# Gate projections written over their inputs' banks, and the order of small steps around the silu group, in a fused attention and state-space kernel

## Chip, cores and metric

The kernel runs on one core of one Trainium2 chip. The metric is the time of one execution on the device in microseconds (us); the time of a version is the median of its runs. An execution recorded by the hardware profiler gives the trace that the profile is made from.

## What is computed

Eight samples of 512 channels and 48x48 = 2304 positions go through two layers, each with a group norm ahead of it and a residual around it. The reference, cut to what matters:

```python
# layer 0: x = x + attention(group_norm(x)), causal linear attention, 8 heads
Q, K = elu(Wq x) + 1, elu(Wk x) + 1
den = 1 / (sum(Q * cumsum(K)) + 1e-10)
out = (Q with causal sum of K V^T) * den
# layer 1: x = x + mamba_groups(group_norm(x)); four groups of 128 channels, one after the other
xp, z = split(u @ Wi.T)                  # 256 channels each
xs = silu(conv4(xp) + bc)
dt, Bm, Cm = split(xs @ Wx.T)            # 8, 16, 16
delta = softplus(dt @ Wdt.T + bdt)
h_t = exp(delta_t * A) * h_{t-1} + delta_t * xs_t * Bm_t    # 16 states per channel
y = (sum(h_t * Cm_t) + xs * Dp) * silu(z)
x_m = y @ Wo.T                           # then mixed with x_i by sigmoid gates of channel means
```

## The kernel before

All data is fp32. Positions are cut into six chunks of 384 columns (LC). The core of the kernel is the recurrence of layer 1. A *job* is one chunk of one group of one sample: 192 jobs, each of 8 *slots*, 1536 slots in all. A slot scans four tiles of 128 partitions by 384 positions. For each of them ScalarE (ACT) computes a *decay*, exp(delta * A), into a bank of PSUM (L819); VectorE (DVE) runs the scan over it (L830) and so frees the bank. DVE also makes most of the products delta*x*B of the next slot (L809), GpSimd (POOL) the rest (L798). POOL then multiplies by C (L846), and TensorE (PE) sums the states into yp (L853). `skip` (L787) puts xs*Dp into yp first.

Six banks of PSUM (BANKS) are shared by everything else: decays, convolutions, projections, attention. `take` gives out a bank from a list, `Banks` holds them for one generator and returns them first in, first out. `ahead(n)` emits decays until n of them are waiting for their scans or no bank is spare; after each scan n is DEPTH = 3, and ahead of the silu and softplus groups n is 5. A bank returned with `late=True` is kept for decays.

Around these slots the rest is emitted by generators that yield a time and a number of banks that they need. The unit of time is a *half*, half a slot: `beside(2k)` runs after the product of slot k and before its scans, `beside(2k+1)` after its second scan. A string like "1" means that many halves after the generator's last step; a pair (t, g) means half t and at least g halves after the last step; "1w" waits for a condition. A generator whose banks are not there is asked again in the next half. The order in which all this is emitted is the order of each engine's queue; it is fixed when the program is built.

What matters around the change:

- `Job.prepare` makes a job's inputs about nine slots ahead. `conv(h)` is four matmuls (L635) of the two halves of channels, `gate(h)` one matmul for z (L646). The *silu group* on ACT is a table load and four activations, L670, L673 (both convolutions), L674 and L675 (both gates); a table load for exp follows (L819). Before the group three banks are held, and `gate(1)` takes one more after the first is freed. Then x_proj (L681) is copied by L686, dt_proj (L694) follows, and the *softplus group* (L705): a table load, two activations, a table load back to exp.
- `chunk(m)` is one chunk of attention for 128 channels. Its steps stand at `at(j)`, j halves after `times[m]`; chunks start 16 halves apart (at least 11). Projections (L288), features on ACT (L300, L301), q on DVE (L345), k (L353), v (L359), the causal sum of k (L364), pr = q times that (L374), transposes of k and v (L381) with their copies (L385, L386), denominators (L393) and the states' sums k v^T (L398) in one bank called `both`, on DVE the reciprocal rd (L401, L402) and the sums into S (L410), rd spread out by ACT (L414) and transposed by PE (L418) into another bank, q scaled by it (L423), scores (L431), mask (L436), output (L445, L449), residual and its statistics (L452, L454).
- `statistics(b)` reads sample b in 24 pieces and takes bn_stats of each (L242); `group_norm` makes a scale and a shift from statistics, by L169 to L195 with two matmuls (L171, L186). It serves both layers.
- `pass_on` brings a stream's next input: ACT scales and norms (L596, L597, L601 or L599, L607), POOL adds (L604, L609, L612). From the second chunk of a group its step stands 30 halves ahead of the job's first slot.
- SyncE (SP) issues all loads and stores in its own order.

Of the kernel before, what the change touches and what calls it, by code (L numbers as in the profile page):

```python
# [9 lines left out]
F32 = mybir.dt.float32  # L10
# [6 lines left out]
P = 128  # L17
T = 128
LC = 384
# [30 lines left out]
def attention_then_mamba_kernel(  # L50
# [17 lines left out]
    nc = tc.nc  # L68
# [92 lines left out]

    def group_norm(stats, n, name, bufs):


        bank = Banks()
        yield "1", 1
        mv = small.tile([P, n, 2], F32, tag=f"mv{n}", name=f"mv_{name}", bufs=1)
        for ct in range(n):
            nc.vector.bn_aggr(mv[:, ct, :], stats[:, ct].rearrange("p c s -> p (c s)"))  # L169
        mean_ps = bank()  # L170
        nc.tensor.matmul(mean_ps[:, 0:n], grp, mv[:, :, 0], start=True, stop=True)  # L171
        yield "1", 0
        gm = small.tile([P, 3, n], F32, tag=f"gm{n}", name=f"gm_{name}", bufs=1)
        nc.vector.tensor_copy(gm[:, 0, :], mean_ps[:, 0:n])
        nc.vector.tensor_sub(gm[:, 1, :], mv[:, :, 0], mean_ps[:, 0:n])
        bank.free()
        if n == 1:
            nc.vector.tensor_scalar(
                gm[:, 2, :], gm[:, 1, :], gm[:, 1, :], mv[:, 0, 1:2], ALU.mult, ALU.add
            )  # L180
        else:
            nc.vector.tensor_mul(gm[:, 2, :], gm[:, 1, :], gm[:, 1, :])
            nc.vector.tensor_add(gm[:, 2, :], gm[:, 2, :], mv[:, :, 1])
        yield "0", 1
        var_ps = bank()
        nc.tensor.matmul(var_ps[:, 0:n], grp, gm[:, 2, :], start=True, stop=True)  # L186
        yield "1", 0
        nc.vector.tensor_scalar_add(gm[:, 2, :], var_ps[:, 0:n], 1e-5)
        bank.free()
        norm = small.tile([P, 3, n], F32, tag=f"norm{n}", name=f"norm_{name}", bufs=bufs)  # L190
        nc.gpsimd.tensor_tensor(norm[:, 0, :], gm[:, 2, :], power[:, 0:n], ALU.pow)
        yield "1", 0
        for i, factor in ((0, -1.0), (1, float(L))):
            for ct in range(n):
                nc.vector.tensor_scalar(  # L195
                    norm[:, 1 + i, ct : ct + 1],
                    gm[:, i, ct : ct + 1],
                    norm[:, 0, ct : ct + 1],
                    factor,
                    ALU.mult,  # L200
                    ALU.mult,
                )
        return norm
# [5 lines left out]
    def statistics(b):  # L209

        xv = x[b].rearrange("(t p) l -> p t l", p=P)
        stats = small.tile([P, 4, NC, 6], F32, tag="stats_a", name=f"stats_a{b}", bufs=1)
        if b == 0:
# [19 lines left out]
        else:  # L233
            for ct in range(4):
                for c in range(NC):
                    yield "2", 0
                    if (ct, c) == (0, 0):
                        nxt = piece(b, 0)
                    xs = nxt
                    i = ct * NC + c + 1  # L240
                    nxt = piece(b, i) if i < 4 * NC else None
                    nc.vector.bn_stats(stats[:, ct, c, :], xs)  # L242
        norms[b] = yield from group_norm(stats, 4, f"a{b}", 2)

# [23 lines left out]
    def chunk(m):  # L268
# [73 lines left out]
        ex = feature(qp, qb)  # L342
        yield at(2), 0
        q = new("q", 2)
        nc.vector.scalar_tensor_tensor(q, ex, 1.0, qp, ALU.min, ALU.add)  # L345
        bank.free()
        yield at(2, 0), 1
        kp, kb = project(1)
        yield at(3), 0
        ex = feature(kp, kb)  # L350
        yield at(4), 0
        k = new("k", 2)
        nc.vector.scalar_tensor_tensor(k, ex, 1.0, kp, ALU.min, ALU.add)  # L353
# [14 lines left out]
        if ksum is not None:  # L368
            kept = new("kept")
            nc.scalar.copy(kept[64:128], kc[64:128])  # L370
            save(ksum[:, cols], kept[64:128])
# [16 lines left out]

        yield at(12), 1
        both = bank()  # L390
# [5 lines left out]
        for i in range(more):  # L396
            for h in heads_of:
                nc.tensor.matmul(ds[h, i, :], kl[:, i, h], v[:, i, h], start=True, stop=True)  # L398
        yield at(14), 0
        rd = small.tile([P, 2 * NT], F32, tag="rd", name=f"rd_{n}", bufs=1)  # L400
# [5 lines left out]
        for i in range(more):  # L406
            if c == 0 and i == 0:
                nc.vector.tensor_copy(S[:, place[1], :], ds[:, 0, :])
            else:
                nc.vector.tensor_add(S[:, place[i + 1], :], S[:, place[i], :], ds[:, i, :])  # L410
        bank.free()
        yield at(15), 0
        rdb = new("rdb", 1, (P, 2 * NT, 64))
        nc.scalar.copy(rdb, rd.unsqueeze(2).to_broadcast([P, 2 * NT, 64]))  # L414
        yield at(16), 1
        rb = bank()[:, 0:LC].rearrange("p (i t) -> p i t", i=NT)
        for i in range(NT):
            nc.tensor.transpose(  # L418
                rb[:, i, :], rdb[:, 2 * i : 2 * i + 2, :].rearrange("p e d -> p (e d)"), ident
            )  # L420
        yield at(18), 0

# [33 lines left out]
        if c + 1 == NC:  # L456
            norm = yield from group_norm(stats, 1, f"m{b}_{o}", 8)
            flush()
            done[b, o] = norm
# [156 lines left out]
    class Job:  # L616
# [6 lines left out]
        def prepare(self):  # L623
# [19 lines left out]

            def gate(h):
                zp = bank()[:, 0:LC]
                nc.tensor.matmul(  # L646
                    zp,
                    wi[:, 256 + h * P : 256 + (h + 1) * P],
                    xi[:, c0 + 3 : c0 + 3 + LC],
                    start=True,  # L650
                    stop=True,
                )
                return zp

# [3 lines left out]
            converting.append(n)  # L658
            yield "1", 1
            xc0 = conv(0)  # L660
            yield "2", 2
            xc1 = conv(1)
            zp0 = gate(0)
            yield "1", 0
            xs = self.xs = mpool.tile([P, 2, LC], F32, tag="xs", name=f"xs_{n}")
# [4 lines left out]
            nc.scalar.activation(xs[:, 0, :], xc0, AF.Silu, bias=pv[:, 0:1])  # L670
            bank.free()
            zp1 = gate(1)
            nc.scalar.activation(xs[:, 1, :], xc1, AF.Silu, bias=pv[:, 1:2])  # L673
            nc.scalar.activation(sz[0], zp0, AF.Silu)  # L674
            nc.scalar.activation(sz[1], zp1, AF.Silu)  # L675
            converting.clear()
            bank.free(3, late=True)
            yield "1", 1
# [65 lines left out]
            for h in range(2):  # L744
                yield "1", 0
                nc.gpsimd.tensor_tensor(delta[:, h, :], delta[:, h, :], xs[:, h, :], ALU.mult)  # L746
            first = 2 * self.start
            yield "2", 0
# [208 lines left out]
    def finale(job):  # L957
# [4 lines left out]
        if job.c == NC - 1:  # L962
            yield from job.stream.pass_on()

    begun, put, counted = 0, 0, list(range(1, B))

    def begin(latest):

        nonlocal begun, put
        while counted and times[parts.index((counted[0], 0, 0))] - 64 <= half_no[0]:  # L970
            tasks.append(Task(statistics(counted.pop(0))))
# [220 lines left out]
```

## Time and profile before

| | |
|---|---|
| median of 3 runs | 9329.64 us (9327.21 to 9330.81) |
| profiled execution | 9323.3 us, its span 9321.5 us |
| granted TensorE clock | 0.948 |
| mean DMA rate | 176 GB/s |
| first scan starts | 222.5 us |
| ACT table loads ahead of L670, L705, L819 | 192, 192, 382, of 1283 ns each |

A line of the costliest groups reads: line, engine, operation, what is written and read, count, then busy time and the mean of one, then the engine's idle time just before these instructions and what ended most of it. A line of waits reads: who waited, for whom, us in total, times, longest. A line of the timeline reads: start, duration, engine, line, operation, and in brackets the idle time before it and what ended it. "DVE u L830" as a cause is the end of a scan, mostly because it frees a bank. A matmul of fp32 stands as two passes in the counts.

### The profile page before, as it was taken

The numbers are of one execution on the slowest core, as the hardware profiler recorded it, in microseconds if no ns is written. First come the engines' busy times: TensorE is split into PE (matmuls) and PEld (weight loads), VectorE is DVE, ScalarE is ACT, GpSimd is POOL, SyncE is SP. The second block draws the span as 40 slices with busy tenths as digits, with TensorE's granted clock in tenths as the row PEclk, the third lists the DMA queues.
The fourth block names the chain that finished last, engine by engine and source line by source line (L and its number), as shares of the span: only waits on it lengthen the run. The fifth ranks groups of instructions, "written<-read, shape, count | busy, mean of one in ns | idle before, by whom it ended". The sixth has DMA issues, their size and how long they took to land.

```text
span 9321.5 us, 120629 instructions
## 1 busy us (share of the span) xinstructions
PE 7735.1 (83%) x35714; PEld 3673.0 (39%) x35714; DVE 8348.4 (90%) x11640; ACT 6580.2 (71%) x12656; POOL 8080.8 (87%) x5635
## 2 busy tenths in 40 slices
PE   7888888888888888888888888888888888888865
PEld 4444444433344444443343444443333434444321
DVE  3899999999999999999999999999999999999997
ACT  3677777777777777777777777776777777777775
POOL 2788888889988898889998888888998888888998
PEclk9999999999999999999999999999999999999977
DMA  6566666667666666666766666667666666666654
GB/s 189 158 169 173 175 174 168 180 189 198 188 169 176 177 179 172 176 183 189 196 182 178 174 175 173 174 170 194 192 184 182 176 176 172 173 171 175 167 153 129
DMA packets 1002899, 1642.84 MB, mean 176 GB/s; under 512 B 138592, under 2 KB 797312, under 8 KB 1002240
## 3 DMA queue, kind: packets, MB, share of 16 engines
q1 hardware_dynamic: 1002240, 1635.13, 64.1%
q8 instruction: 283, 4.64, 0.2%
q14 instruction: 376, 3.08, 0.1%
HBM read 1309.06 MB, written 325.58 MB: 175 GB/s over the span
## 4 chain that ended last, share of the span: by engine, by line
DVE 39%; ACT 20%; PE 18%; issue 7%; DMA 7%; POOL 6%; SPq 2%; DVEq 0%; POOLq 0%; ACTq 0%
DVE u L830 23%; DVE u L809 8%; PE bank L288 7%; ACT bank L819 6%; PE bank L635 4%; POOL u L846 4%; ACT L819 3%; PE yp L853 3%; PE bank L646 2%; ACT L705 2%; DMA B<-scr 2%; DMA C<-scr 1%; ACT bank L301 1%; ACT delta L705 1%; DVE sm L436 1%
## 5 line engine op out<-in xcount | busy, mean ns | idle before, releaser
L830 DVE TENSOR_TENSOR_SCAN u<-bank,u 128x385 f32<-128x385 f32 (+1 forms) x6144 | 5475.1, 938 | 530.5 <-ACT bank L819 503.2
L846 POOL TENSOR_TENSOR u<-u,C 128x1536 f32<-128x1536 f32 x1536 | 4885.1, 3180 | 219.5 <-DVE u L830 112.6
L819 ACT ACTIVATE bank<-dr,av 128x385 f32<-128x385 f32 (+1 forms) x6144 | 3431.3, 579 | 1556.9 <-DVE u L830 1113.3
L853 PE MATMUL yp<-u,cst 128*64 128x384 f32 x12288 | 2429.9, 514 | 282.7 <-ACT yp L787 146.3
L798 POOL TENSOR_TENSOR u<-B,dxr 128x512 f32<-128x512 f32 x1536 | 1959.9, 1276 | 22.4 <-DMA dxr<-xscr 19.0
L288 PE MATMUL bank<-xn,wq_sb 128*128 128x384 f32 x4608 | 1855.1, 552 | 48.8 <-DVE u L830 31.7
L809 DVE TENSOR_TENSOR u<-B,dxp 128x1024 f32<-128x1024 f32 x1536 | 1834.7, 1195 | 10.7 <-ACT dxp L782 10.7
L853 PEld LDWEIGHTS yp<-u,cst 128*64 128x64 f32 x12288 | 788.3, 139 | 1476.6 <-issue 903.5
L635 PE MATMUL bank<-xi,wk 128*128 128x384 f32 x3072 | 1118.2, 507 | 280.1 <-ACT kl L385 172.7
L288 PEld LDWEIGHTS bank<-xn,wq_sb 128*128 128x128 f32 x4608 | 929.1, 212 | 862.9 <-issue 215.1
L635 PEld LDWEIGHTS bank<-xi,wk 128*128 128x128 f32 x3072 | 563.7, 193 | 862.2 <-ACT kl L385 254.1
L844 POOL COPY state<-u 128x4 f32<-128x4 f32 x1280 | 243.8, 190 | 740.6 <-DVE u L830 738.0
L300 ACT ACTIVATE ex<-bank,bqkv_sb 128x384 f32<-128x384 f32 x384 | 221.3, 576 | 561.6 <-PE bank L288 539.2
L787 ACT ACTIVATE yp<-xs,pv 128x384 f32<-128x384 f32 x384 | 223.4, 582 | 405.7 <-DVE yz L865 405.7
L819 ACT ACT_TABLE_LOAD x382 | 490.1, 1283 | 6.7
L746 POOL TENSOR_TENSOR delta<-delta,xs 128x384 f32<-128x384 f32 x384 | 385.8, 1005 | 95.5 <-DMA dscr<-delta 84.3
L418 PE MATMUL bank<-cst,rdb 128*128 128x128 f32 x576 | 112.7, 310 | 426.1 <-DVE u L830 334.7
L694 PE MATMUL bank<-dbc,wd 9*128 9x384 f32 x768 | 316.3, 524 | 65.1 <-ACT dbc L686 29.0
L646 PE MATMUL bank<-xi,wi 128*128 128x384 f32 x768 | 297.8, 500 | 59.8 <-ACT xs L670 59.8
L871 PE MATMUL bank<-yz,wo 128*128 128x384 f32 x768 | 297.6, 509 | 34.1 <-DVE yz L865 19.4
L449 PE MATMUL bank<-sm,v 128*64 128x128 f32 x2304 | 257.2, 301 | 42.4 <-DVE u L830 40.6
L418 PEld LDWEIGHTS bank<-cst,rdb 128*128 128x128 f32 x576 | 66.8, 153 | 558.9 <-ACT xb L601 272.5
(109 smaller groups left out, 7860.3 us busy)
## 6 DMA issues: line engine op xcount, KB each, us to landing
B<-scr SPq DMA_DIRECT2D x1536, 192.0 KB
C<-scr SPq DMA_DIRECT2D x1536, 192.0 KB
xn<-xn SPq DMA_DIRECT2D x192, 768.0 KB
dr<-dscr SPq DMA_DIRECT2D x768, 192.0 KB
dxr<-xscr SPq DMA_DIRECT2D x768, 192.0 KB
dscr<-delta SPq DMA_DIRECT2D x192, 384.0 KB
xscr<-delta SPq DMA_DIRECT2D x192, 384.0 KB
xn<-in_x SPq DMA_DIRECT2D x48, 768.0 KB
```

Source lines behind the costliest of these rows:

```text
L288: nc.tensor.matmul(ps, wq_sb[:, kt, j * 512 + o * P : j * 512 + (o + 1) * P], xn[:, kt, :], start=(kt == 0), stop=(kt == 3),)
L635: nc.tensor.matmul(xc, wk[:, k, h * P : (h + 1) * P], xi[:, c0 + k : c0 + k + LC], start=(k == 0), stop=(k == 3),)
L646: nc.tensor.matmul(zp, wi[:, 256 + h * P : 256 + (h + 1) * P], xi[:, c0 + 3 : c0 + 3 + LC], start=True, stop=True,)
L694: nc.tensor.matmul(vp, wd[32:41, h * P : (h + 1) * P], dbc[32:41, :], start=True, stop=True)
L746: nc.gpsimd.tensor_tensor(delta[:, h, :], delta[:, h, :], xs[:, h, :], ALU.mult)
L798: nc.gpsimd.tensor_tensor(u[:, :, :, 1 + LC - TAIL :], self.B[s % 4][:, :, cols].unsqueeze(2).to_broadcast(shape), self.dxr[s // 4][:, :, ...
L809: nc.vector.tensor_mul(u[:, :, :, 1 : 1 + LC - TAIL], self.B[s % 4][:, :, cols].unsqueeze(2).to_broadcast(shape), self.dxp.unsqueeze(1).to ...
L819: nc.scalar.activation(dA[:, cols], self.dr[h][:, g, cols], AF.Exp, scale=self.w[6][:, 2 * h + g, q + j : q + j + 1],)
L830: nc.vector.tensor_tensor_scan(u[:, j, g, cols], dA[:, cols], u[:, j, g, cols], 0.0, ALU.mult, ALU.add,)
L846: nc.gpsimd.tensor_tensor(h, h, self.C[s % 4].unsqueeze(2).to_broadcast([P, NG, 2, LC]), ALU.mult)
L853: nc.tensor.matmul(self.yp[g * 64 : g * 64 + 64, 0:LC], pair_sum, u[:, j, g, 1:], start=False, stop=(s % 4 == 3 and j == NG - 1), skip_gro ...
L871: nc.tensor.matmul(self.xm[:, 0:LC], self.w[2][:, h, :], self.yz[:, h, :], start=(h == 0), stop=(h == 1),)
```

## The change

The number of instructions of every engine stays as it is, and so does what they compute.

- In `prepare` the gates take no banks of their own. Gate h writes the bank of convolution h, after the silu that reads it. Both gates now stand behind the second convolution and behind their silus; two banks are held and freed in place of four. The steps of the convolutions and of the silu group stand at fixed halves (21, 19 and 18 ahead of the job's first half).
- In `chunk` the second projection is emitted ahead of the q product, which moves from half 2 to half 3; two projections then hold banks at once. The denominators and sums move from half 12 to half 10, with no gap asked, and rd and the sums into S from 14 to 12. The bank `both` isn't freed after them: the transposed rd is written over it, and it is freed after q is scaled, at half 16 in place of 18.
- Statistics of a sample (from the third on) take one piece per 16 halves, at fixed halves, over a longer time, with the load two halves ahead; for the second sample a piece per half. The statistics' tile has two buffers. The group norm of layer 1 has its steps at halves 28 to 31 of its chunk.
- `kept` shares a buffer with `before` of the attention.

```diff
-    def group_norm(stats, n, name, bufs):
+    def group_norm(stats, n, name, bufs, places=("1", "1", "0", "1", "1")):
...
-        yield "1", 1
+        yield places[0], 1
...
         else:
-            for ct in range(4):
-                for c in range(NC):
-                    yield "2", 0
-                    if (ct, c) == (0, 0):
-                        nxt = piece(b, 0)
-                    xs = nxt
-                    i = ct * NC + c + 1
-                    nxt = piece(b, i) if i < 4 * NC else None
-                    nc.vector.bn_stats(stats[:, ct, c, :], xs)
+            when = begins[b] + b % 2
+            for i in range(4 * NC):
+                yield (when - 2, 1) if b > 1 else "1", 0
+                xs = piece(b, i)
+                yield (when, 1) if b > 1 else "1", 0
+                nc.vector.bn_stats(stats[:, i // NC, i % NC, :], xs)
+                when += PERIOD
...
         ex = feature(qp, qb)
-        yield at(2), 0
-        q = new("q", 2)
+        yield at(2), 1
+        kp, kb = project(1)
+        yield at(3), 0
+        q, k = new("q", 2), new("k", 2)
         nc.vector.scalar_tensor_tensor(q, ex, 1.0, qp, ALU.min, ALU.add)
         bank.free()
-        yield at(2, 0), 1
-        kp, kb = project(1)
-        yield at(3), 0
         ex = feature(kp, kb)
...
-            kept = new("kept")
+            kept = new("before")
...
-        yield at(12), 1
+        yield at(10, 0), 1
         both = bank()
...
-        yield at(14), 0
+        yield at(12), 0
         rd = small.tile([P, 2 * NT], F32, tag="rd", name=f"rd_{n}", bufs=1)
...
-        bank.free()
-        yield at(15), 0
+        yield at(13), 0
         rdb = new("rdb", 1, (P, 2 * NT, 64))
...
-        yield at(16), 1
-        rb = bank()[:, 0:LC].rearrange("p (i t) -> p i t", i=NT)
+        yield at(14), 0
+
+        rb = both[:, 0:LC].rearrange("p (i t) -> p i t", i=NT)
...
-        yield at(18), 0
+        yield at(16), 0
...
-            norm = yield from group_norm(stats, 1, f"m{b}_{o}", 8)
+            norm = yield from group_norm(
+                stats, 1, f"m{b}_{o}", 8, [(times[m] + j, 1) for j in (28, 29, 29, 30, 31)]
+            )
...
-            def gate(h):
-                zp = bank()[:, 0:LC]
+            def gate(h, zp):
...
-            yield "1", 1
+            first = 2 * self.start
+            yield (first - 21, 0), 1
             xc0 = conv(0)
-            yield "2", 2
+            yield (first - 19, 2), 1
             xc1 = conv(1)
-            zp0 = gate(0)
-            yield "1", 0
+            yield (first - 18, 1), 0
...
             nc.scalar.activation(xs[:, 0, :], xc0, AF.Silu, bias=pv[:, 0:1])
-            bank.free()
-            zp1 = gate(1)
+
+            gate(0, xc0)
             nc.scalar.activation(xs[:, 1, :], xc1, AF.Silu, bias=pv[:, 1:2])
-            nc.scalar.activation(sz[0], zp0, AF.Silu)
-            nc.scalar.activation(sz[1], zp1, AF.Silu)
+            gate(1, xc1)
+            nc.scalar.activation(sz[0], xc0, AF.Silu)
+            nc.scalar.activation(sz[1], xc1, AF.Silu)
             converting.clear()
-            bank.free(3, late=True)
+            bank.free(2, late=True)
...
+    begins = {}
+    for b in counted:
+        first = times[parts.index((b, 0, 0))]
+        begins[b] = (first - 20) // PERIOD * PERIOD - 4 * NC * PERIOD - 2 if b > 1 else first - 64
...
-        while counted and times[parts.index((counted[0], 0, 0))] - 64 <= half_no[0]:
+        while counted and begins[counted[0]] - 4 <= half_no[0]:
```

More of the change, by code (lines that the diff above doesn't have):

```diff
@@ L171, in group_norm @@
         nc.tensor.matmul(mean_ps[:, 0:n], grp, mv[:, :, 0], start=True, stop=True)
-        yield "1", 0
+        yield places[1], 0
         gm = small.tile([P, 3, n], F32, tag=f"gm{n}", name=f"gm_{name}", bufs=1)
@@ L183, in group_norm @@
             nc.vector.tensor_add(gm[:, 2, :], gm[:, 2, :], mv[:, :, 1])
-        yield "0", 1
+        yield places[2], 1
         var_ps = bank()
         nc.tensor.matmul(var_ps[:, 0:n], grp, gm[:, 2, :], start=True, stop=True)
-        yield "1", 0
+        yield places[3], 0
         nc.vector.tensor_scalar_add(gm[:, 2, :], var_ps[:, 0:n], 1e-5)
@@ L191, in group_norm @@
         nc.gpsimd.tensor_tensor(norm[:, 0, :], gm[:, 2, :], power[:, 0:n], ALU.pow)
-        yield "1", 0
+        yield places[4], 0
         for i, factor in ((0, -1.0), (1, float(L))):
@@ L211, in statistics @@
         xv = x[b].rearrange("(t p) l -> p t l", p=P)
-        stats = small.tile([P, 4, NC, 6], F32, tag="stats_a", name=f"stats_a{b}", bufs=1)
+        stats = small.tile([P, 4, NC, 6], F32, tag="stats_a", name=f"stats_a{b}", bufs=2)
         if b == 0:
@@ L342, in chunk @@
         ex = feature(qp, qb)
-        yield at(2), 0
-        q = new("q", 2)
+        yield at(2), 1
+        kp, kb = project(1)
+        yield at(3), 0
+        q, k = new("q", 2), new("k", 2)
         nc.vector.scalar_tensor_tensor(q, ex, 1.0, qp, ALU.min, ALU.add)
         bank.free()
-        yield at(2, 0), 1
-        kp, kb = project(1)
-        yield at(3), 0
         ex = feature(kp, kb)
         yield at(4), 0
-        k = new("k", 2)
         nc.vector.scalar_tensor_tensor(k, ex, 1.0, kp, ALU.min, ALU.add)
@@ L652, in gate @@
                 )
-                return zp
             while converting or not st.scaled:
@@ L658, in prepare @@
             converting.append(n)
-            yield "1", 1
+            first = 2 * self.start
+            yield (first - 21, 0), 1
             xc0 = conv(0)
-            yield "2", 2
+            yield (first - 19, 2), 1
             xc1 = conv(1)
-            zp0 = gate(0)
-            yield "1", 0
+            yield (first - 18, 1), 0
             xs = self.xs = mpool.tile([P, 2, LC], F32, tag="xs", name=f"xs_{n}")
@@ L746, in prepare @@
                 nc.gpsimd.tensor_tensor(delta[:, h, :], delta[:, h, :], xs[:, h, :], ALU.mult)
-            first = 2 * self.start
             yield "2", 0
```

## Prediction

> **What bounds the kernel now.** I read the busy shares first, then what VectorE (DVE) waited for in the steady part, then the timeline around one such wait. Of the page, the shares and the costliest group:
>
> ```profile
> PE 7735.1 (83%) x35714; PEld 3673.0 (39%) x35714; DVE 8348.4 (90%) x11640; ACT 6580.2 (71%) x12656; POOL 8080.8 (87%) x5635
> L830 DVE TENSOR_TENSOR_SCAN u<-bank,u 128x385 f32<-128x385 f32 (+1 forms) x6144 | 5475.1, 938 | 530.5 <-ACT bank L819 503.2
> ```
>
> DVE is the bound: 8348 of 9321.5 us. The change moves DVE work but adds and removes none (the built order of both kernels has 11,450 DVE instructions), so the time can only move through the 973 us in which DVE idles. The waits of DVE between 230 and 9300 us name the idle time (total us, times, longest):
>
> ```profile
> DVE u L830 <- ACT bank L819: 503.2, 194, 4.7
> DVE q L345 <- ACT bank L301: 108.1, 54, 4.2
> DVE k L353 <- ACT bank L301: 56.0, 135, 1.0
> DVE gm_m L188 <- PE bank L186: 29.4, 31, 1.1
> ```
>
> There are 192 jobs and 194 waits of a scan for its decay: one per job, 2.6 us each. One of them, on ScalarE (ACT), then DVE, then TensorE (PE):
>
> ```profile
> 4054.83 0.58 ACT L819 ACTIVATE bank<-dr,av 128x385 f32<-128x385 f32 x1 [0.26 <-DVE u L830]
> ...
> 4055.54 1.28 ACT L670 ACT_TABLE_LOAD   x1
> 4056.84 0.58 ACT L670 ACTIVATE xs<-bank,pv 128x384 f32<-128x384 f32 x1
> ...
> 4058.42 0.49 ACT L675 ACTIVATE sz<-bank 128x384 f32<-128x384 f32 x1
> ...
> 4060.23 2.10 ACT L819 ACTIVATE bank<-dr,av 128x385 f32<-128x385 f32 x4
> ...
> 4067.87 1.28 ACT L705 ACT_TABLE_LOAD   x1
> ...
> 4071.35 0.59 ACT L819 ACTIVATE bank<-dr,av 128x385 f32<-128x385 f32 x1
> 4074.67 0.58 ACT L300 ACTIVATE ex<-bank,bqkv_sb 128x384 f32<-128x384 f32 x1 [2.73 <-PE bank L288]
> ```
> ```profile
> 4057.53 0.95 DVE L830 TENSOR_TENSOR_SCAN u<-bank,u 128x385 f32<-128x385 f32 x1
> 4060.85 0.96 DVE L830 TENSOR_TENSOR_SCAN u<-bank,u 128x385 f32<-128x385 f32 x1 [2.36 <-ACT bank L819]
> ...
> 4075.73 0.56 DVE L345 SCALAR_TENSOR_TENSOR q<-ex,bank 128x384 f32<-128x384 f32 x1 [3.05 <-ACT bank L301]
> ```
> ```profile
> 4057.47 0.91 PE L646 MATMUL bank<-xi,wi 128*128 128x384 f32 x2 [0.19 <-ACT xs L670]
> 4058.22 0.72 PE L393 MATMUL bank<-cst,pr 128*128 128x2 f32 x6
> ...
> 4069.71 0.55 PE L418 MATMUL bank<-cst,rdb 128*128 128x128 f32 x3 [3.75 <-ACT delta L705]
> ```
>
> The reader is to see two chains. In the first, ACT makes no decay for 4.69 us (4055.54 to 4060.23), while DVE has only the decays made before. In the second, PE stands 3.75 us at the transposes of L418, for want of a bank; the projection queued behind them comes late, ACT waits at L300, and DVE waits at L345. The second group of this kind on ACT (softplus, 4067.87 to 4071.35, 3.48 us in every job) costs DVE nearly nothing: 0.14 us on average before its scan.
>
> **What the Trainium skill says.** "ScalarE: Activation LUTs", What ACT_TABLE_LOAD costs, gives 1283 ns for a load and about 1380 ns of drain beside it. The trace agrees on the load and shows no drain: the next activation starts 0.01 us after it, so I price a switch at 1.28 us. "PSUM — Partial Sum Buffer", Specifications, gives 8 banks and PSUM as all that TensorE writes; with dxp and yp in two, six are left, as in the code. "Perfetto Trace Analysis", Optimization Strategy, says that consistent bubbles can mean that there isn't enough PSUM. The trace agrees: the bubble is there once a job, and behind L418 stands a bank.
>
> **The rule for a group.** The last decay ahead of a group waits for the bank that an earlier scan frees. Call that scan's end R. Need is the time from R until the first decay behind the group is done; cover is the DVE work from R to the scan that takes it. DVE waits need less cover. In the built order of before, R lies four scans ahead of that scan at the silu group, in all 190 groups in the steady part. Measured over them: 6.55 us from R to the scan, 2.61 idle, so cover 3.94 (three scans of 0.86, a product of 1.12 and small ones). In its commonest form (L385 and L386 queued ahead) the need is 6.59.
>
> **Part 1, the silu group.** (a) Need. Today ACT waits for one gate only; L675 starts 1.00 us after the first silu ends in nearly all groups. In the change both gates write banks that the silus have just read. Gate 0 can't begin before the first silu ends, and gate 1 follows. A matmul of 128x384 is two passes of 0.322 us start to start (L288 and L635 back to back), so the fourth activation starts 0.64 us later. Moreover the order puts the denominators and sums (L393, L398) between the second convolution and gate 0, where today gate 0 stands. They take 1.06 us (4058.22 until L681 starts at 4059.28). The convolution starts when L385 has freed its bank, and its last pass has been issued 2.67 us later; with 1.06 gate 0 starts at 3.73. The first silu ends at 3.20, and would let it start at 3.31. That is 0.43 more. Need: 6.59 + 0.64 + 0.43 = 7.66. Bounds: 0.64 alone if PE has the sums done early, 1.5 if the gates meet a late convolution; I take 1.07. (b) Cover. R stays four scans ahead in 176 of 190. The order now has L401, L402 and the L410s in this stretch in 182 groups (0.85 us: 4061.72 to 4062.61 less gaps) and 144 pieces of bn_stats instead of 19 (0.5 each): 0.81 + 0.33 = 1.14 per group, so 5.1. (c) Wait: 7.69 (with 0.03 to the scan's start) - 5.1 = 2.6, as today. 190 x 2.6 = 492 against 495: the cover that is gained is spent on the longer group. Effect about -3 us.
>
> **Part 2, the softplus group.** Nothing in its lines changes, but its banks do. Today one bank is spare there: the sums' bank is back, and that of L418 isn't taken yet. A fourth decay lies ahead of the group, and R to the scan is five scans and two products. In the change the sums' bank is held from phase 10 until L423. With two for softplus, three decays are all that six banks hold, and the order shows R only four scans ahead in 177 of 190. Cover is a product, three scans and L423: 1.12 + 3 x 0.86 + 0.45 = 4.15. Need: the decay 0.52, then what the order queues behind it (L596, L597, L601: 0.51 + 0.51 + 0.69, all three in 110 groups, two in 30, one in 7), the group 3.48, the next decay 0.58, two handovers 0.06: 6.35, 5.66, about 5.3, or 4.64 with none (35). Waits: 110 x 2.2 + 30 x 1.5 + 7 x 1.2 + 35 x 0.5 = 312 us, less the 26 of today: +286. Bounds: the group alone, with nothing queued ahead of it, is 190 x 0.5 - 26 = +70; ACT coming 0.5 us late to that decay adds 95 to the 286, so +380.
>
> **Part 3, the second chain.** L418 writes the bank it already holds, so PE no longer stands there (L418 waited 335 us for scans, 86 for L705). The first projection's bank comes from the scan after R, two us behind R; the projection (eight passes, 2.7 us) is done near R + 4.8, and ACT comes to L300 after R + 6.4. The q product (L345) moves a slot part later too. So 108 + 56 go, and I leave 10: -154 us. Next late is ACT at the decay that stands behind L300 and L787; it is done 3.7 us after the softplus scan, and needed at 5.5. Bounds -100 and -164.
>
> **Part 4, the statistics.** The norm's L188 (29 us) moves to where DVE waits in any case: -29, or 0. The pieces' loads on SP are issued two half-slots ahead as before, among the B and C loads; today bn_stats waits 0.3 us in all after the start, in every phase. Priced at 0. If SP is blocked, up to 2 us of it falls into the silu wait. The 140 us of idle before the first scan are PE's and DMA's; +-10.
>
> **Sum.** -3 + 286 - 154 - 29 = +100 us against the profiled execution (9323.3 us, span 9321.5): 9423. The median of the runs is 6.3 higher, so 9430.
>
> **Rivals.** *Faster.* Were the softplus stretch hidden, what is left is -186: 9144. One mechanism: the decay ahead of L596 must be made from a bank free before R. It turns the sign where the new wait falls under 1.0 us a group (186 / 190) instead of 1.6. For it: today's group of the same length is hidden. Against it: the banks in the order. *About even.* The silu group takes the 0.64 alone (wait 2.16, -82 us) and some softplus waits shrink: 9335. For it: PE waits 0.8 us on average ahead of L646 today. Against: conv and silu start from the same L385, so the sums can't be done early. *Slower still.* The gates hold PE's queue, the gathers of L853 stand behind them, yp and L787 come late and hold ACT: 0.5 us more per job, 9525. Against: ACT idles 406 us at L787 today and DVE doesn't feel it.
>
> **Chances.** Forecast 0.60 (9370 to 9490 by itself), even 0.17, faster 0.13, slower still 0.10. A change of about 0.2% (19 us) is what a measurement here can tell. Slower by more: 0.60 + 0.10 + 0.02 of the even case; within: 0.11; faster: 0.13 + 0.04. The range 9320 to 9520 leaves out the faster rival and half of the slowest.
>
> **What would show it.** Right: DVE waits for L819's successor about 380 times, half of them behind a softplus group at 1.6 us; the silu waits still near 2.5 us; gate 0 late behind the sums; no wait at the q product; no PE wait at the rb transposes. Wrong: fewer than 250 such waits, or silu waits under 2 us.

## The result and the profile after

| | before | after |
|---|---|---|
| median | 9328.49 us (4 runs) | 9653.74 us (4 runs, 9645.74 to 9666.77) |
| ratio | | 1.035, 95% interval 1.0332 to 1.0368 |
| profiled execution, its span | 9323.3, 9321.5 us | 9666.8, 9665.0 us |
| DVE busy, idle | 8348, 933 us | 8388, 1237 us |
| granted TensorE clock | 0.948 | 0.926 |

The change makes the kernel 325 us slower. The forecast had the direction, and 100 us. (The idle time is the sum of the gaps ahead of DVE's instructions, the 17 us ahead of its first among them.)

The page of the changed kernel, the lines that answer to those of before (scan and decay are now L826 and L815):

```profile
PE 7992.1 (83%) x35714; PEld 3742.1 (39%) x35714; DVE 8388.3 (87%) x11640; ACT 6628.2 (69%) x12656; POOL 8074.7 (84%) x5635
L826 DVE TENSOR_TENSOR_SCAN u<-bank,u 128x385 f32<-128x385 f32 (+1 forms) x6144 | 5497.5, 939 | 668.7 <-ACT bank L815 638.2
```

What DVE waited for over the whole run:

```profile
DVE u L826 <- ACT bank L815: 638.2, 340, 2.3
DVE rd L397 <- PE bank L394: 223.3, 190, 10.4
DVE k L349 <- ACT bank L299: 117.4, 91, 3.3
DVE fg L878 <- PE bank L867: 51.2, 30, 2.3
...
DVE gm_m L188 <- PE bank L186: 13.5, 31, 3.7
...
DVE q L345 <- ACT bank L299: 7.8, 7, 3.6
```

The scans wait 340 times and not 194, at most 2.3 us at a time. Two waits are new, at the reciprocal rd (for the sums) and at fg (for the output projection), and the q waits are gone.

One job shows every term. First ACT, from the silu group (4021.73) over the softplus group (4034.72) to the k features (4049.57):

```profile
4021.73 0.58 ACT L666 ACTIVATE xs<-bank,pv 128x384 f32<-128x384 f32 x1
...
4023.89 0.49 ACT L671 ACTIVATE sz<-bank 128x384 f32<-128x384 f32 x1 [1.11 <-PE bank L643]
...
4032.48 0.58 ACT L815 ACTIVATE bank<-dr,av 128x385 f32<-128x385 f32 x1 [0.27 <-DVE u L826]
4033.00 0.60 ACT L594 ACTIVATE fu<-fu,wt 128x384 f32<-128x384 f32 x1
...
4034.72 1.28 ACT L702 ACT_TABLE_LOAD   x1
...
4038.20 1.09 ACT L815 ACTIVATE bank<-dr,av 128x385 f32<-128x385 f32 x2
...
4049.57 0.58 ACT L298 ACTIVATE ex<-bank,bqkv_sb 128x384 f32<-128x384 f32 x1 [4.42 <-PE bank L286]
```

Then DVE in the same job:

```profile
4023.06 0.17 DVE L397 TENSOR_SCALAR rd<-bank 128x6 f32<-128x6 f32 x1 [0.66 <-PE bank L394]
...
4026.95 0.96 DVE L826 TENSOR_TENSOR_SCAN u<-bank,u 128x384 f32<-128x384 f32 x1 [1.57 <-ACT bank L815]
...
4038.82 0.96 DVE L826 TENSOR_TENSOR_SCAN u<-bank,u 128x385 f32<-128x385 f32 x1 [2.23 <-ACT bank L815]
...
4050.63 0.56 DVE L349 SCALAR_TENSOR_TENSOR k<-ex,bank 128x384 f32<-128x384 f32 x1 [1.95 <-ACT bank L299]
```

And PE:

```profile
4022.94 1.56 PE L643 MATMUL bank<-xi,wi 128*128 128x384 f32 x4
...
4034.48 2.85 PE L286 MATMUL bank<-xn,wq_sb 128*128 128x384 f32 x8 [1.33 <-DVE u L826]
...
4041.41 1.65 PE L867 MATMUL bank<-yz,wo 128*128 128x384 f32 x2 [3.44 <-DVE yz L861]
4042.99 2.83 PE L849 MATMUL yp<-u,cst 128*64 128x384 f32 x8
4045.75 3.79 PE L286 MATMUL bank<-xn,wq_sb 128*128 128x384 f32 x8
```

The reader is to see a chain that the prediction didn't have. DVE waits 2.23 us behind the softplus group, so the gated y (yz) is late; PE, which reached the output projection L867 early, stands 3.44 us for it. What PE does next runs slowly: the eight matmuls of L849, which sum the states into yp, take 2.83 us, where others of them take 1.51, and the k projection takes 3.79, where the q projection of the same size took 2.85. Over the whole run PE is busy 7992 us with the same 35,714 passes that took 7735 before. So ACT gets the k projection late (4.42 us of wait) and DVE waits once more, at k.

Where DVE's idle time went, by place, summed over the profiled executions (us). A group's place reaches from the end of the scan R, as the prediction defines it (four scans ahead), to the scan that takes the first decay behind the group; waits at q, k and fg stand in a row of their own:

| place | before | after | difference | forecast |
|---|---|---|---|---|
| silu groups, with rd and the norm steps in them | 531 | 563 | +32 | -32 |
| softplus groups | 26 | 323 | +297 | +286 |
| products q, k, fg | 214 | 176 | -38 | -154 |
| all else, the start among it | 162 | 175 | +13 | 0 |
| DVE busy | 8348 | 8388 | +40 | 0 |

Idle and busy together give 344 us, the difference of the spans. The busy 40 are 18 us of longer durations and 22 us of lost overlap: two DVE instructions in a row overlap by some 0.08 us in the records, and where there is a gap between them they don't. There are some 250 gaps more, 200 of them over 0.15 us.

### The profile page after: what moved, and what is told of

It is laid out like the page before. It is cut to its first block, busy times and chain, and to the rows that moved or that the text cites. A ratio compares the mean times of both kernels' runs of the same rounds, so it can differ in the third digit from the quotient of the medians.

```text
span 9665.0 us, 120018 instructions
## 1 busy us (share of the span) xinstructions
PE 7992.1 (83%) x35714; PEld 3742.1 (39%) x35714; DVE 8388.3 (87%) x11640; ACT 6628.2 (69%) x12656; POOL 8074.7 (84%) x5635
## 4 chain that ended last, share of the span: by engine, by line
DVE 32%; ACT 22%; PE 20%; POOL 9%; issue 8%; DMA 6%; SPq 2%; DVEq 0%; POOLq 0%; ACTq 0%
DVE u L826 19%; DVE u L805 7%; ACT bank L815 7%; PE bank L633 6%; POOL u L842 5%; ACT L815 4%; PE bank L286 4%; PE yp L849 3%; PE bank L643 3%; DMA C<-scr 3%; ACT L702 2%; POOL u L794 2%; ACT delta L702 1%; DVE yz L861 1%; PE bank L867 1%
## 5 line engine op out<-in xcount | busy, mean ns | idle before, releaser
L826 DVE TENSOR_TENSOR_SCAN u<-bank,u 128x385 f32<-128x385 f32 (+1 forms) x6144 | 5497.5, 939 | 668.7 <-ACT bank L815 638.2
L815 ACT ACTIVATE bank<-dr,av 128x385 f32<-128x385 f32 (+1 forms) x6144 | 3433.3, 579 | 1561.9 <-DVE u L826 1338.2
L849 PE MATMUL yp<-u,cst 128*64 128x384 f32 x12288 | 2697.8, 549 | 157.3 <-POOL u L842 124.1
L286 PE MATMUL bank<-xn,wq_sb 128*128 128x384 f32 x4608 | 1784.9, 533 | 129.5 <-DVE u L826 100.8
L849 PEld LDWEIGHTS yp<-u,cst 128*64 128x64 f32 x12288 | 860.0, 147 | 1504.5 <-issue 979.8
L286 PEld LDWEIGHTS bank<-xn,wq_sb 128*128 128x128 f32 x4608 | 902.3, 207 | 1092.5 <-DVE u L826 376.5
L867 PE MATMUL bank<-yz,wo 128*128 128x384 f32 x768 | 376.6, 583 | 399.2 <-DVE yz L861 387.6
L815 ACT ACT_TABLE_LOAD x381 | 488.8, 1283 | 6.7
L691 PE MATMUL bank<-dbc,wd 9*128 9x384 f32 x768 | 340.4, 554 | 104.3 <-DVE u L826 70.4
L867 PEld LDWEIGHTS bank<-yz,wo 128*128 128x128 f32 x768 | 145.1, 210 | 565.0 <-DVE yz L861 486.6
L377 PE MATMUL bank<-cst,vT 128*128 128x128 f32 x576 | 102.6, 287 | 223.8 <-DVE pr L370 200.3
```

The costliest lines, as they stand in the source:

```text
L286: nc.tensor.matmul(ps, wq_sb[:, kt, j * 512 + o * P : j * 512 + (o + 1) * P], xn[:, kt, :], start=(kt == 0), stop=(kt == 3),)
L691: nc.tensor.matmul(vp, wd[32:41, h * P : (h + 1) * P], dbc[32:41, :], start=True, stop=True)
L815: nc.scalar.activation(dA[:, cols], self.dr[h][:, g, cols], AF.Exp, scale=self.w[6][:, 2 * h + g, q + j : q + j + 1],)
L826: nc.vector.tensor_tensor_scan(u[:, j, g, cols], dA[:, cols], u[:, j, g, cols], 0.0, ALU.mult, ALU.add,)
L849: nc.tensor.matmul(self.yp[g * 64 : g * 64 + 64, 0:LC], pair_sum, u[:, j, g, 1:], start=False, stop=(s % 4 == 3 and j == NG - 1), skip_gro ...
L867: nc.tensor.matmul(self.xm[:, 0:LC], self.w[2][:, h, :], self.yz[:, h, :], start=(h == 0), stop=(h == 1),)
```

## The experiments

Theory A is that the loss comes from the decay that no longer lies ahead of the softplus group. Its rivals: B, the gates hold TensorE's queue; C, the order of work in TensorE's queue makes VectorE wait; D, TensorE has no time left, whatever its order; E, TensorE runs slower after it has stood still. Ratios are to the kernel before on the same chip. Differences in us from the changed kernel are differences of medians; the kernel before measured 9325 to 9332 us beside the different runs, so some 10 us of such a difference mean nothing.

**pass_on later** (the changed kernel, with)

```diff
-                    yield (first - 30, 1), 0
+                    yield (first - 28, 1), 0
```

> The changed kernel with one edit: the ACT steps of pass_on stand 28 halves ahead of the job in place of 30, so that they are queued behind the softplus group and not ahead of it. Theory A (decays: the loss is VectorE waiting behind the softplus group, because only three decays lie ahead of it and pass_on's three activations are queued between the last of them and the group): the wait per group falls from 2.2 us (with three activations) to 0.5, 226 us in all, and about 40 us of waits that follow from it; 60 us may come back because the activations now stand ahead of another decay: 9390 to 9480 us. Theory B (TensorE: the gates hold its queue and it runs at a lower clock, and VectorE waits for what comes late from it): the order of these ACT steps matters little, 9600 to 9660 us.

Measured: 9582.77 us, ratio 1.0267 (1.0252 to 1.0283), 71 us under the changed kernel. Idle time at the softplus groups fell from 323 to 110 us, 213 of the 226 expected. But DVE waited at k more than before the edit:

```profile
DVE u L826 <- ACT bank L815: 439.3, 370, 2.3
DVE rd L397 <- PE bank L394: 223.4, 190, 10.2
DVE k L349 <- ACT bank L299: 211.1, 139, 3.4
```

So A has the wait right to 0.1 us a group, but only a third of it comes through, and the time misses A's range: behind it stands another chain.

**q scaled before the softplus group** (the changed kernel, with)

```diff
-        yield at(16), 0
+        yield at(15), 0
         nc.vector.tensor_mul(q, q, rb.rearrange("p i t -> p (i t)"))
```

> The changed kernel with one edit: q is scaled by the transposed reciprocal one half earlier, so that the bank of denominators and reciprocal is free when the softplus group is emitted, and the order has a fourth decay ahead of the group (waiting for the scaling of q). Theory A: need 6.9 us from the scan, cover about 6.6, so the softplus wait nearly goes: 270 of 308 us, 9350 to 9400 us with the waits that follow. Theory B: the granted clock and the gates are as before, 9600 to 9660 us.

Measured: 9505.65 us, 1.0183 (1.0166 to 1.02), 148 us under the changed kernel. At the softplus groups 78 us of idle time are left, 245 less. Other waits of DVE grew: at k to 140 us, at fg to 81, at L188 to 43. One bank freed some 2.2 us sooner, seen from the start of the group, is worth 1.5% here, and again not all of it arrives; A had forecast 9350 to 9400 us.

**Gates alone** (the kernel before, with)

```diff
-            def gate(h):
-                zp = bank()[:, 0:LC]
+            def gate(h, zp):
...
-            yield "2", 2
+            yield "2", 1
             xc1 = conv(1)
-            zp0 = gate(0)
...
-            bank.free()
-            zp1 = gate(1)
+            gate(0, xc0)
...
+            gate(1, xc1)
-            nc.scalar.activation(sz[0], zp0, AF.Silu)
-            nc.scalar.activation(sz[1], zp1, AF.Silu)
+            nc.scalar.activation(sz[0], xc0, AF.Silu)
+            nc.scalar.activation(sz[1], xc1, AF.Silu)
...
-            bank.free(3, late=True)
+            bank.free(2, late=True)
```

> The kernel before with one part of the change alone: the gates write the banks of the convolutions, two banks in place of four. The order now has four decays ahead of the silu group in 159 of 190 groups. Theory A: the group is 0.64 us longer (the second gate follows the first on TensorE) but the cover grows from 3.9 to 5.8 us, so the silu wait falls from 2.7 to about 1.4 us: 9329 - 250 = 9080 to 9130 us. Theory B (gates behind the silus hold TensorE's queue, and that is what costs): slower than before, 9400 us or more.

Measured: 9340.75 us, 1.0008 (0.9999 to 1.0016): no difference. B is out: the gates by themselves don't make the kernel slow. A's forecast of 9080 to 9130 us fails too. The group is 0.69 us longer on average (4.76 to 5.45), about as said. The fourth decay ahead is there, but the last of them begins only 1.2 us earlier: ACT itself is busy, copying k and v (L385, L386) right ahead of the last two decays in 121 of 190 groups. With the longer group, and 0.14 us more of cover, that leaves 0.63 us a group: 531 us of idle time became 412. Waits elsewhere took this back, mostly those at k (156 us for 71) and at rd (69, of which 41 lie within the 412).

**The sums' bank alone** (the kernel before, with)

```diff
-        bank.free()
         yield at(15), 0
...
-        yield at(16), 1
-        rb = bank()[:, 0:LC].rearrange("p (i t) -> p i t", i=NT)
+        yield at(16), 0
+        rb = both[:, 0:LC].rearrange("p (i t) -> p i t", i=NT)
```

> The kernel before with another part alone: the transposed reciprocal is written over the bank of denominators and sums, which is held until q is scaled; times as before. The order has three decays ahead of the softplus group in 180 groups in place of four. Theory A: softplus waits of about 2.7 us in 91 groups, 2.0 in 24, 1 or less in the rest, 340 us in all, less up to 160 us of waits at the q and k products, since TensorE no longer stands for a bank: 9480 to 9540 us. Theory B: the part only frees TensorE, so it gains: 9180 to 9250 us.

Measured: 9645.90 us, 1.0333 (1.0317 to 1.0348). That is nearly the whole loss, with this part alone, and 106 us more than A's range. Its waits (scan, k and q):

```profile
DVE u L829 <- ACT bank L818: 913.7, 374, 4.7
DVE k L353 <- ACT bank L301: 90.5, 99, 5.7
DVE q L345 <- ACT bank L301: 72.9, 40, 6.0
```

Idle time at the softplus groups is 412 us; in 91 of them it is 3.0 us each. PE no longer stands for a bank at the transposes, and the q waits fall by 69 us; the k waits rise by 20. The freed PE gains 50 us, not 160: it now stands at the output projection, further on in its own queue.

```profile
PE bank L870 <- DVE u L829: 310.6, 159, 2.9
...
PE bank L870 <- DVE yz L864: 102.9, 138, 4.0
```

**k projection ahead of the output projection** (the changed kernel, with)

```diff
         qp, qb = project(0)
+        yield at(0, 0), 1
+        kp, kb = project(1)
         yield at(1), 0
         ex = feature(qp, qb)
-        yield at(2), 1
-        kp, kb = project(1)
         yield at(3), 0
```

> The changed kernel with one edit: the second projection is emitted right behind the first, one and a half slots earlier, so that on TensorE it stands ahead of the output projection, which waits for the gated y. Theory C (order on TensorE: freed from its wait at the transposes, TensorE now stands 2.4 us per job at the output projection, with the k projection queued behind it, and VectorE pays at the k product): the k waits fall from 117 us to under 30 and the wait of the output projection from 388 us to under 200: 9530 to 9580 us. Theory D (TensorE has no time left, whatever its order): k waits go down but waits at other products come in their place, 9630 to 9670 us.

Measured: 9641.19 us, 1.0335 (1.0318 to 1.0353), 13 us under the changed kernel. The k waits are gone, and fg waits 154 us for 51. TensorE stands 67 us for yz at the output projection and not 388; it stands at the scores (L427, 413 us). C is right about who waits behind whom, and wrong about what it is worth: the wait got another name, and the time lies in D's range.

**Sums behind the gates** (the changed kernel, with)

```diff
-        yield at(10, 0), 1
+        yield at(11, 0), 1
         both = bank()
...
-        yield at(12), 0
+        yield at(13), 0
         rd = small.tile([P, 2 * NT], F32, tag="rd", name=f"rd_{n}", bufs=1)
...
-        yield at(13), 0
+        yield at(14), 0
         rdb = new("rdb", 1, (P, 2 * NT, 64))
...
-        yield at(14), 0
+        yield at(14, 0), 0
         rb = both[:, 0:LC].rearrange("p (i t) -> p i t", i=NT)
```

> The changed kernel with the denominators and sums emitted one half later, behind the gates, and the reciprocal and sums on VectorE one half later too. Theory A: the silu group on ScalarE is 0.45 us shorter (5.89 to 5.44), since gate 0 no longer waits for the sums; and as the sums' bank is taken later, the order has a fourth decay ahead of the group, cover 7.2 us against a need of about 8.0: the idle time of VectorE per silu group falls from 3.0 to about 1.1 us. 350 us less, of which up to 100 may come back at the k product: 9300 to 9400 us. Rival (as in the gates-only run, ScalarE is late itself, and the waits are only renamed): the group is shorter, but the time falls by less than 120 us.

Measured: 9394.49 us, 1.0069 (1.0053 to 1.0084), 259 us under the changed kernel. The time lies in A's range, and its rival is out. The silu group takes 5.40 us for 5.89; its idle time falls from 563 to 320 us, and the softplus groups keep theirs (some 350 us). What is left at the silu groups over the forecast of 1.1 us each is in two waits for TensorE in this stretch, rd and the norm's mean:

```profile
DVE u L826 <- ACT bank L815: 350.7, 202, 3.4
DVE rd L397 <- PE bank L394: 144.2, 150, 4.2
DVE gm_m L174 <- PE bank L171: 103.1, 30, 4.0
```

**Norm steps as before** (the changed kernel, with)

```diff
-            norm = yield from group_norm(
-                stats, 1, f"m{b}_{o}", 8, [(times[m] + j, 1) for j in (28, 29, 29, 30, 31)]
-            )
+            norm = yield from group_norm(stats, 1, f"m{b}_{o}", 8)
```

> The changed kernel with the steps of the layer 1 group norm as before. Theory C: the variance matmul (L186) no longer takes a bank that the softplus group holds, so TensorE doesn't stand 200 us there, and the 52 us in which VectorE waits at the fg product (30 times about 1.7) go; up to 29 us may come back at L188: 9590 to 9640 us. Rival: the fg waits come from the output projection's wait in every job, and stay; within 20 us of the changed kernel.

Measured: 9676.63 us, 1.0371 (1.0356 to 1.0387), 23 us over the changed kernel. The fg waits are gone (1 us), as C said, but the rd waits grew from 223 to 319 us, and the time misses C's range. Taking the later norm steps away gains nothing here.

**TensorE kept busy** (the changed kernel, with three matmuls ahead of each output projection whose results nobody reads)

```diff
             self.xm = self.bank()
+            for _ in range(3):
+                nc.tensor.matmul(self.xm[:, 0:LC], ident, cst[:, 0:LC], start=True, stop=True)
```

> The changed kernel with three matmuls more ahead of every output projection, into the bank that the projection then overwrites: 576 matmuls of 128x384 that compute nothing needed, about 1.9 us of TensorE per job, placed where it stands waiting. Theory E (the clock: standing for two to three us lowers TensorE's rate for what follows, and that is what makes the k projection late): the k waits fall from 117 to about 60 us, the k projection takes 2.9 us and not 3.8, and the time falls by 30 to 80 us: 9570 to 9620 us. Theory D (TensorE has no time left): the added work comes through as later projections, k and fg waits grow, 9700 us or more.

Measured: 9628.54 us, 1.0320 (1.0305 to 1.0335): 25 us faster than the changed kernel with 576 matmuls more, 9 us outside E's range. The granted clock went from 0.926 to 0.948, and TensorE's stands for yz at the output projection from 388 us to 107. DVE at fg and k, in that kernel:

```profile
DVE fg L880 <- PE bank L869: 121.2, 43, 4.1
...
DVE k L349 <- ACT bank L299: 17.3, 10, 3.3
```

The k waits went from 117 to 17 us, further than E had it, and 70 us came back at fg. By D, which has no time left on TensorE, the kernel would have been slower: D is out. The rate can be read in the traces. Taking two successive passes of 384 columns of one line, the time between their starts, by the length of TensorE's last stand and the time since it ended:

```
kernel           stands of 2.5 to 4 us    passes 0-3 us after    passes 8 us and more after
before                     73                 0.63 to 0.64              0.322
changed                   136                 0.63 to 0.69              0.322
kept busy                  52                 0.63 to 0.69              0.322
(medians in us; after stands of 1 to 1.5 us, 0.32 throughout, in all three)
```

The border isn't sharp. Of the passes within 3 us after stands of 2 to 2.5 us, 32% were over 0.5 us apart before, 58% in the changed kernel and 7% in the one kept busy.

**The rest alone** (the kernel before, with the order of the q product, the spread statistics, the later norm steps and the shared buffer of the change; the steps of the convolutions as before)

> The kernel before with what is left of the change when the gates and the sums' bank stay as before: the second projection ahead of the q product, the pieces of statistics spread out, the group norm's later steps, the shared buffer. Theory A+C: bn_stats gives the silu group 0.33 us more cover (60 us), L188 no longer waits (25 us), and the q waits (142 us) turn partly into k and fg waits; no decay is lost: 9180 to 9290 us. Rival (the loss is spread over all parts): slower than before, 9350 us or more.

Measured: 9356.01 us, 1.0030 (1.0019 to 1.0042), 31 us slower, where a gain of 40 us and more was forecast. The q waits went from 142 to 20 us, fg rose from 1 to 103, and a wait of the norm for POOL (L195) from 1 to 38. The idle time at the silu groups fell by 22 us, but only because L188 (29 us) no longer waits there. The scan's own wait rose from 496 to 505 us, though 132 pieces of bn_stats stand in that stretch and not 18.

**All but the sums' bank** (the changed kernel, with)

```diff
-        yield at(10, 0), 1
+        yield at(12), 1
         both = bank()
...
-        yield at(12), 0
+        yield at(14), 0
...
+        bank.free()
-        yield at(13), 0
+        yield at(15), 0
...
-        yield at(14), 0
-        rb = both[:, 0:LC].rearrange("p (i t) -> p i t", i=NT)
+        yield at(16), 1
+        rb = bank()[:, 0:LC].rearrange("p (i t) -> p i t", i=NT)
...
-        yield at(16), 0
+        yield at(18), 0
```

(with the convolutions' steps relative to each other, as before)

> The changed kernel without its part on the sums' bank: gates, projections, statistics and norm steps as in the change; denominators, sums, reciprocal and its transposes at the times and in the banks of before. Theory A: the loss of the change lies in this one part; gates alone were +8 us, the rest alone as in the run beside it, and the two add up: within 40 us of that run, 9170 to 9300 us. Rival (the parts hurt each other): 9400 us or more.

Measured: 9319.34 us, 0.9994 (0.9988 to 1.0001). Without this part the change costs nothing: taking it away gains 334 us, more than the whole loss of 325. (The time is over A's range of 9170 to 9300, but within 40 us of the run beside it, as A said.) Gates (+8), sums' bank (+313) and the rest (+31), each alone, add to 352; the parts nearly add up. What was taken away here is two things, the bank held until q is scaled and the sums a half or more earlier, ahead of the gates, and these two don't add: the bank alone costs 313 us in the kernel before, sums behind the gates give 259 in the changed one, and both together give 334.

**Three mends together** (the changed kernel with the sums behind the gates, q scaled at half 15, norm steps as before: the diffs above)

> The changed kernel with three edits together: sums behind the gates and the reciprocal one half later (9394 us alone), q scaled one half earlier so that a fourth decay lies ahead of the softplus group (148 us alone), group norm steps as before. Theory A: the first two add up, less what returns at the k and fg products: idle time at the softplus groups under 100 us, 9230 to 9300 us. Theory D (TensorE is what limits there): the waits are renamed once more, 9380 us or more.

Measured: 9310.07 us, 0.9985 (0.9978 to 0.9992), 344 us under the changed kernel, and 0.15% under the kernel before. Idle time at the softplus groups is 54 us, at the silu groups 346. A had forecast 9230 to 9300 us and D 9380 or more; the time lies just over A's range. DVE now waits most at

```profile
DVE k L349 <- ACT bank L299: 265.7, 173, 3.6
DVE rd L397 <- PE bank L394: 251.2, 176, 6.2
```

**Three mends, TensorE kept busy** (the same, with the three matmuls)

> The kernel of the run beside it with three matmuls more ahead of every output projection, which compute nothing needed. Theory E (clock): where TensorE stands less before the k projection, VectorE waits less at the k product, as in the changed kernel, where it gave 26 us: 20 to 80 us faster than the run beside it. Theory D: 20 us or more slower.

Measured: 9237.82 us, 0.9901 (0.9887 to 0.9916), 72 us faster than the run beside it. Its k waits are a third of that one's:

```profile
DVE rd L397 <- PE bank L394: 261.9, 177, 6.7
DVE k L349 <- ACT bank L299: 90.0, 141, 3.6
DVE fg L878 <- PE bank L867: 84.2, 84, 5.5
```

The granted clock is 0.970. It is the fastest version, 1% under the kernel before, and 72 of these 87 us come from work that computes nothing. E forecast 20 to 80 us.

## Why the prediction was right or wrong

**Where the forecast missed.** It had +100 us for the spans, which differ by 344. Of the 244 between them 116 lie in part 3, 64 in part 1 with the norm's credit, 40 in DVE's busy time, which had no term, 13 in all else and 11 in part 2.

**Part 2, softplus: right.** By what is queued between the last decay and the group, the forecast had waits of 2.2, 1.5, 1.2 and 0.5 us; the trace has 2.21 (110 groups), 1.63 (30), 1.22 (7) and 0.49 (30). The part forecast +286 and measured +297. The run of the sums' bank alone and the run without it show that this edit carries the loss.

**Part 3, the second chain: failed.** The step was "Next late is ACT at the decay that stands behind L300 and L787", with the q and k waits gone. Next late was TensorE itself. Its waits, before and then in the changed kernel:

```profile
PE bank L418 <- DVE u L830: 334.7, 149, 2.8
...
PE bank L418 <- ACT delta L705: 86.2, 28, 3.8
...
PE bank L871 <- DVE yz L865: 19.4, 10, 2.4
```
```profile
PE bank L867 <- DVE yz L861: 387.6, 159, 4.7
PE bank L633 <- ACT kl L381: 240.0, 164, 1.6
```

Where it had stood 421 us at the transposes for scans and L705, it now stands 388 us for the gated y, in front of the k projection; that wait was 19 us. In the run of the sums' bank alone 414 us stand at the same place. The prediction followed the q projection as far as ACT and never asked what lies behind it in TensorE's own queue. Then the rate: behind a stand of more than 2.5 us most passes of the next 3 us come at half rate, and there were some 150 such stands for some 85. The Trainium skill has a halving of this kind ("TensorE: Matmul & The Clock Gate", What's actually happening: the clock is halved after an idle window of about 3.4 us and needs as long a busy one to come back). The passes at 0.634 us for 0.322 agree; here they came already after stands of 2.5 to 4 us, and in part after 2 to 2.5. The prediction used 0.322 everywhere. Together: q -134, k +46, fg +50, in all -38 for -154.

**Part 1, silu: the mechanism right, the sizes short.** The wait "as today" was 2.6 us; DVE is idle 3.0. Over the 176 groups in which R lies four scans ahead, the need, forecast at 7.69 us from the end of scan R to the scan behind the group, measured 7.95. The group is 5.89 where 5.75 was forecast, and the last decay ahead of it starts 0.85 after R, not 0.72. The cover is 4.96, not 5.1. Of the 527 us of idle time of these groups 183 stand at rd, where DVE waits for the sums, which the forecast counted as work. The decay comes later still, so these waits should cost nothing by themselves; no run tests that. It does split the wait: the scan itself waits 1.84 us on average, which by the words of the prediction ("silu waits under 2 us") was a sign of being wrong. The credit of 29 us at L188 came in only in part: L188 still waits 13.5 us, and the norm's mean (L174) went from 2.4 to 8.8. Together this makes +32 for -32.

**Part 4 and the sum.** Statistics cost nothing that the runs show, as priced; in the run of the rest alone they gained nothing either, where 60 us were expected of them. Not in the sum at all were the 40 us of DVE busy time, more than half of them overlap lost, and the start (rd waits 32 us there).

**Rivals.** "Slower still" looked at the right place, TensorE's own queue, with the wrong carrier: it had the gates hold the queue, and the gates alone cost nothing. The "even" and "faster" cases fell with the fourth decay, as the order had said.

What stays open: how much of the k and fg waits is the rate and how much the order. The two runs with added matmuls show that the rate matters (25 and 72 us). How far a version without stands would go was not tried, and neither were the added matmuls in the kernel before. The fixed places of the convolutions' steps were never run by themselves: the runs of the gates, the sums' bank and the rest alone, and the run without the sums' bank, all have them as before.

## What to carry to other kernels

Count banks by how long they are held, not by how many a step takes: a bank kept across a table switch takes a buffer away from the engine that must be ahead there, and the built order shows it before any run. When a wait of an engine goes, read on in that engine's own queue to the next thing that waits, and ask what it holds up; here the two edits that took the softplus wait away gave a third and three fifths of it (71 of 213 us, 148 of 245), since DVE's next waits grew. Time a stage by its stretch of need against cover: that gave the softplus waits to 0.13 us or better.

## What the runs showed of the hardware that had not been expected

- TensorE ran at half rate after standing: fp32 passes of 384 columns came 0.634 us apart for 0.322, for about 3 us after stands of over 2.5 us, and next to never after stands of 1 to 1.5 us. 576 matmuls of no use made one kernel 72 us faster and another 25.
- No time for a drain shows beside the 1283 ns of a table load: the next activation starts 0.012 us after it, and a softplus group took 3.48 us (median of 190) from its table load to the next decay, with two loads and two activations in it.
- Two DVE instructions in a row overlap by some 0.08 us in the records; with a wait between them they don't, so that by these records a wait costs that much more than it lasts.
